# The first spreading of a graph kernel: five buffers of evicted rows, and slot numbers and rows of x asked for further ahead

## The chip, the cores and the metric

The kernel runs on one core of a Trainium2 chip. The metric is the device time of one execution in microseconds (us). The core has five engines that matter here: TensorE (PE, matrix multiplications; PEld are its weight loads), VectorE (DVE), ScalarE (ACT), GpSimd (POOL) and SyncE (SP, which here only issues transfers), and 16 DMA engines, which move data between the main memory (DRAM) and the on-chip memory (SBUF). TensorE writes its results into PSUM, from where VectorE or ScalarE copies ("evicts") them into SBUF.

## The reference

Two layers of a graph network over N = 32768 nodes with D = 128 features and E = 524288 edges, src to dst. Both need sums over edges:

```python
src, dst = edge_index
agg = jax.ops.segment_sum(x[src], dst, num_segments=N)      # layer 0
h = (1.0 + eps) * x + agg
h = relu(h @ W_loc1 + b_loc1) @ W_loc2 + b_loc2
h_local = _bn(x + h, g1, beta1)
... attention over 64 blocks of 512 nodes, feed-forward, norms
for _ in range(3):                                          # layer 1
    ... attention to 512 keys
    agg = zeros_like(x).at[row].add((dinv[:, None] * x)[col])
    x = 0.5 * x + 0.5 * (retrieved - 0.2 * (x - dinv[:, None] * agg))
```

The case concerns the first half of layer 0's `x[src]`: bringing every row of x to the places where the edges that start at it will be summed.

## The kernel before

**The exchange.** A sum over edges is done in two halves. The nodes are cut into NW = 256 windows of P = 128. In the first half, the *spreading*, each window of 128 source rows is multiplied with 0/1 matrices, so that rows come out in the order in which the receivers want them. Each window has 2 x KS = 12 groups of 128 slots (SL = 1536 slots). Edges that find no place in this grid are fetched one by one in the second half. In the second half, each receiving window loads its slots and sums them with other 0/1 matrices. The spread rows go through a DRAM array, `slots_d`, of 256 windows x 1.18 MB, in bf16; a float32 row is carried as three bf16 parts, hence ROW = 3 x 128 = 384 elements.

**The stages.** First comes half of layer 0's attention with the sorting of edges beside it, then the stage of this case, `spread_x` (L1812 to L1886), then a small verdict (`grid.verdict`, whether all edges fit) on which a branch depends, and then `layer0_grid` and `layer1_grid`. `layer0_grid` sums what spread_x wrote, and `layer1_grid` has its own spreadings, which use the same helper `Exchange.spread` from pools of two buffers.

**One window in spread_x.** The order of all instructions is written out by hand (`tc.manual_schedule`), and each engine works through its own in that order. For window w, of block b = w // 4, `ex.spread` runs for m = 0 to 5 (L1443 to L1456):

- two matmuls (L1448) of one group of 128 slots each, from the 0/1 matrix `picks[w]` and the three bf16 parts of the window's rows, into a PSUM tile `exp`, of which there are three;
- one eviction of both groups (L1453) into `y_o`, a tile of 2 x 6 x 384 bf16 elements in each of 128 partitions, that is 9216 bytes. Mostly ScalarE does it; VectorE does m = 2 of all windows and m = 5 of odd ones, that is 3 of 12 in a pair;
- after m = 2 and after m = 5, a store of half of `y_o` to `slots_d` (L1456), issued by SP. The pool `l0e` has two buffers of `y_o`, so the first eviction of window w cannot start before both stores of window w-2 have landed.

The 0/1 matrix of the *next* window is made by VectorE in between. A `row_of` transfer (L1833 to L1838) copies the 1536 slot numbers of one window from a row in DRAM to all 128 partitions, as a `band` (384 KB in SBUF). For odd windows VectorE compares the whole band at once with the partition number (`pick_b`, L1844), after m = 1. For even windows TensorE spreads 512 slot numbers at a time over the partitions (`row_p`, L1423) and VectorE compares them in PSUM (`pick`, L1848), after m = 1, 3 and 5. `row_of(w + 2)` is called at the start of odd w; its pool has two band buffers.

`load(b)` (L1823) asks for a block of four windows of x (256 KB, `xe`, three buffers), at the start of block b-2. ScalarE and VectorE split each block into its three bf16 parts during the block before (`split_steps`, L1386 to L1399), and SP stores these to a table. SP issues the loads of x, the bands, the stores of slots and the stores of the table, in program order, on one queue.

**Beside it** runs a sort of the edges that found no place (`sort_on`, `grid.build_more`), metered at 0.28 us of estimated VectorE time for each m. Its steps are VectorE's min and max over `more_a` and `more_b` (L96, L98), with some transposes.

Of the kernel before, what the change touches and what calls it, by code (L numbers as in the profile page):

```python
# [9 lines left out]
F32 = mybir.dt.float32  # L10
I32 = mybir.dt.int32
BF16 = mybir.dt.bfloat16
# [8 lines left out]
P = 128  # L21
D = 128
BLK = 512
NCH = BLK // P
# [7 lines left out]
KS = 6  # L32
# [10 lines left out]
ROW = 3 * D  # L43
# [866 lines left out]
def tile_gnn_resnorm(ctx: ExitStack, tc: tile.TileContext, a: dict, out: bass.AP):  # L910
# [68 lines left out]
    w = {}  # L979
# [342 lines left out]
    SL = 2 * KS * P  # L1322
# [5 lines left out]
    def grid_consts(pool):  # L1328
        gc["iota1"] = pool.tile([P, P], BF16, name="iota1")
        nc.vector.tensor_scalar(gc["iota1"], iota, 1.0, None, op0=OP.add)  # L1330
        gc["lane1"] = pool.tile([P, 1], F32, name="lane1")
        nc.vector.tensor_scalar(gc["lane1"], lane_f, 1.0, None, op0=OP.add)
        gc["down"] = pool.tile([P, P], BF16, name="down")
        nc.vector.tensor_copy(gc["down"], gc["lane1"].to_broadcast([P, P]))
        gc["ident"] = pool.tile([P, P], BF16, name="ident_b")
        nc.vector.tensor_copy(gc["ident"], ident)

    def rows_of(t, i):

        return t.rearrange("(b c p) d -> b p c d", c=NCH, p=P)[i]  # L1340
# [14 lines left out]
    class Exchange:  # L1355
# [8 lines left out]
        def __init__(self, key, slots, table):  # L1364
            self.grid, self.slots, self.table = grid.out[key], slots, table
            self.width = table.shape[1]
            self.bands = {}

        def load_rows(self, pool):
            self.row = pool.tile([P, 2, SL], BF16, name="row")  # L1370
            nc.sync.dma_start(self.row.rearrange("p h f -> p (h f)"), self.grid["row"])
# [71 lines left out]
        def spread(self, wp, pp, tag, w, pick, r, m, st, to_dve):  # L1443

            ps = pp.tile([P, 2, BLK], F32, name="exp", tag=tag)
            for j in range(2):
                o = (2 * m + j) * P
                nc.tensor.matmul(ps[:, j, :ROW], pick[:, o:o + P], r, start=True, stop=True)  # L1448
            if m == 0:
                st["y"] = wp.tile([P, 2, KS, ROW], BF16, name="y_o")  # L1450
            y = st["y"]
            dst = y.rearrange("p h r d -> p (h r) d")[:, 2 * m:2 * m + 2, :]
            (nc.vector.tensor_copy if to_dve else nc.scalar.copy)(dst, ps[:, :, :ROW])  # L1453
            if m % 3 == 2:
                h = m // 3
                nc.sync.dma_start(self.slots[h][:, w, :], y[:, h].rearrange("p r d -> p (r d)"))  # L1456
# [355 lines left out]
    def spread_x():  # L1812

        ex = Exchange("dst", slots_d[1], rows_d[T_STEPS])
        with tc.tile_pool(name="l0r", bufs=1) as gp, tc.tile_pool(name="l0e", bufs=2) as wp, \
                tc.tile_pool(name="l0e_p", bufs=2, space=PSUM) as p_k, \
                tc.tile_pool(name="l0e_e", bufs=3, space=PSUM) as p_e:
            grid_consts(gp)
            ex.load_rows(gp)
            xb, rows, ends, picks, bands, y = {}, {}, {}, {}, {}, {}  # L1820
            more = {"steps": grid.build_more(lane, Bank(p_k, "row_p")), "quota": 0.0}

            def load(b):  # L1823
                if b < NB:
                    xb[b] = wp.tile([P, NCH, D], F32, name="xe", bufs=3)
                    nc.sync.dma_start(xb[b], rows_of(a["x"], b))

            def split(b):
                if b < NB:
                    x = xb.pop(b)  # L1830
                    rows[b], ends[b] = ex.split_steps(wp, b, x, x)

            def row_of(w):  # L1833

                if w < NW:
                    bands[w] = wp.tile([P, SL], BF16, name="band")
                    src = ex.grid["row"][w % P:w % P + 1, w // P * SL:(w // P + 1) * SL]
                    nc.sync.dma_start(bands[w], src.to_broadcast([P, SL]))  # L1838

            def pick(w, j):  # L1840
                if w < NW and w % 2:
                    if j == 0:
                        picks[w] = wp.tile([P, SL], BF16, name="pick_b")
                        nc.vector.tensor_scalar(picks[w], bands.pop(w), gc["lane1"], None, op0=OP.is_equal)  # L1844
                elif w < NW:
                    if j == 0:
                        picks[w] = wp.tile([P, SL], FP8, name="pick")
                    nc.vector.tensor_scalar(picks[w][:, j * BLK:(j + 1) * BLK], ex.listed_row(p_k, "row_p", w, j),  # L1848
                                            gc["lane1"], None, op0=OP.is_equal, saturate=False)

            def sort_on():

                more["quota"] += MORE
                while more["steps"] is not None and more["quota"] > 0:
                    us = next(more["steps"], None)
                    if us is None:
                        more["steps"] = None
                    elif us < 0:
                        more["quota"] = 9 * us * MORE
                    else:  # L1860
                        more["quota"] -= us

            with tc.manual_schedule():
                load(0)
                load(1)
                split(0)
                for f in ends.pop(0):
                    f()
                row_of(1)
                for j in range(SL // BLK):  # L1870
                    pick(0, j)
                for w in range(NW):
                    b, c = divmod(w, NCH)
                    if w % 2:
                        row_of(w + 2)
                    if c == 0:
                        load(b + 2)
                        split(b + 1)
                    for m in range(KS):
                        ex.spread(wp, p_e, "exp", w, picks[w], rows[b][:, c, :], m, y, m == 2 or (m == 5 and w % 2))  # L1880
                        if m % 2:
                            pick(w + 1, m // 2)
                        if m == 3 and b + 1 in ends:
                            ends[b + 1][c]()
                        sort_on()
                for _ in more["steps"] or ():  # L1886
                    pass
# [125 lines left out]
    def layer1_grid(v_d, s3, c3):  # L2013

        exs = [Exchange("src", slots_d[t % 2], rows_d[t]) for t in range(T_STEPS)]
        with tc.tile_pool(name="l1g", bufs=1) as gp:
# [79 lines left out]
            def emit(t, b, st, wp, p_e, p_s, p_tr, share):  # L2096
# [39 lines left out]
                def spread(n):  # L2136
# [5 lines left out]
                    if m == KS - 1:  # L2142
                        del picked[i]

                places = [(n, lambda n=n: spread(n)) for n in range(NCH * KS)]
                return places + [(0, lambda: scores(0)), (3, lambda: scores(1)), (5, lambda: turn(0)),
                                 (6, lambda: scores(2)), (8, lambda: turn(1)), (9, lambda: scores(3)),
# [145 lines left out]
    with tc.tile_pool(name="atg", bufs=1) as gp, tc.tile_pool(name="ata", bufs=2) as ap, \  # L2293
# [4 lines left out]
        with tc.manual_schedule():  # L2298
# [13 lines left out]
            for us in edges or ():  # L2312
                pass
    spread_x()
    grid.verdict(flag)

# [47 lines left out]
```

## Time and profile before

| | |
|---|---|
| median of three runs | 13041.76 us (13023.18 to 13044.78) |
| the profiled execution | 13037.29 us |
| its span in the profile | 13035.5 us |
| mean granted TensorE clock, whole span | 0.947 |
| first L1448 matmul of spread_x | starts at 2344.3 us |
| last L1453 eviction of spread_x | ends at 3577.1 us |
| spread_x between these | 1233 us, VectorE busy 1081.7, ScalarE 928.2, TensorE 823.4 us, DMA share 0.89, 323 GB/s |
| first slots asked for by layer0_grid (L1461) | 3601.6 us |

The profile is of one execution. A line of a wait list names the engine and line that waited, then what it waited for; then follow the total of these waits in us, their number, and the longest. A line of the timeline has the start and the duration in us, the engine, the line, the operation, what it writes and reads, the number of merged instructions and, in brackets, how long the engine stood idle before it and what ended that. A line of stretches has the stretch, its length, the busy time and number of instructions of each engine, the granted TensorE clock (1.00 is full speed), the mean busy share of the 16 DMA engines (it passes 1 a little in places) and the GB/s that they moved.

The durations of one instruction in the stage, as the profile has them:

| line | engine | what | count | mean |
|---|---|---|---|---|
| L1453 | ACT | eviction into y_o, 128x768 | 1152 | 811 ns, less where they follow each other closely |
| L1453 | DVE | the same | 384 | 950 ns |
| L1848 | DVE | pick from row_p, 128x512 | 383 | 745 ns |
| L1844 | DVE | pick_b from a band, 128x1536 | 128 | 614 ns |
| L1448 | PE | exp, 128x384 | 3072 | 344 ns |
| L1423 | PE | row_p, 128x512 | 382 | 409 ns |

### The profile page before, as it was taken

What the parts mean: (1) busy time and instruction counts of PE and PEld (TensorE: products, weight loads), DVE (VectorE), ACT (ScalarE), POOL (GpSimd) and SP (SyncE); (2) the same over time, 40 slices, a digit from 0 to 9 for tenths busy, and PEclk for the clock granted to TensorE, in tenths of its full rate; (3) what the DMA queues carried; (4) which work ended last, traced back from release to release, by engine and by line L of the source; (5) the groups of instructions that cost most, each with busy time, mean ns of one, the idle gap of its engine ahead of it and who ended that gap; (6) DMA issues with size and microseconds to landing.
All of it is one profiled execution on the core that took longest, in us unless ns stands there. A gap on an engine that the chain in (4) does not pass through costs nothing. (4 is left out here: it accounts for less than half of the span.)

```text
span 13035.5 us, 164718 instructions
## 1 busy us (share of the span) xinstructions
PE 11183.2 (86%) x57832; PEld 5535.3 (42%) x57832; DVE 9515.6 (73%) x15195; ACT 6579.4 (50%) x10238; POOL 6154.3 (47%) x5525
## 2 busy tenths in 40 slices
PE   7798798666689999989997999999899999866666
PEld 2233233232244444444443555555455555433333
DVE  7978977798778888688886666666566666566666
ACT  4455355677723333478885666666566666500000
POOL 0083085000077777100003666666566666577777
PEclk9899899899999999999999999999999999987787
DMA  1000000788899999678888999999999999988887
GB/s 43 11 14 20 10 15 19 257 325 324 328 323 341 335 343 343 234 283 309 310 307 312 403 399 400 399 395 400 350 401 398 397 398 400 362 291 290 291 289 253
DMA packets 1410556, 3689.71 MB, mean 283 GB/s; under 512 B 219826, under 2 KB 634706, under 8 KB 1408562
## 3 DMA queue, kind: packets, MB, share of 16 engines
q1 hardware_dynamic: 969712, 2969.23, 60.2%
q0 software_dynamic: 252608, 520.41, 12.4%
q10 hardware_dynamic: 187394, 189.42, 4.4%
q8 instruction: 458, 7.50, 0.2%
q14 instruction: 384, 3.15, 0.1%
HBM read 2175.76 MB, written 1502.58 MB: 282 GB/s over the span
## 5 line engine op out<-in xcount | busy, mean ns | idle before, releaser
L1470 POOL DMA_INDIRECT listed<-rows,other x5120 | 5146.5, 1005 | 4164.4 <-issue 3156.1
L1453 ACT CAST y_o<-exp 128x768 bf16<-128x768 f32 x4224 | 3233.0, 806 | 1148.2 <-PE exp L1448 790.5
L1495 PEld LDWEIGHTS <-oh 128*128 128x128 bf16 x19456 | 1973.3, 102 | 2489.3 <-issue 1421.8
L1448 PE MATMUL exp<-rows,pick 128*128 128x384 bf16 x10752 | 2420.8, 327 | 385.2 <-ACT y_o L1453 223.0
L1495 PE MATMUL seg<-y_i,oh 128*128 128x384 bf16 x12288 | 2565.5, 345 | 21.0 <-DMA y_i<-slots 19.8
L1453 DVE CAST y_o<-exp 128x768 bf16<-128x768 f32 x1920 | 1830.3, 953 | 678.4 <-PE exp L1448 558.1
L1495 PE MATMUL seg<-listed,oh 128*128 128x384 bf16 (+1 forms) x5120 | 1242.6, 335 | 676.4 <-DMA listed<-rows,other 616.1
L1448 PEld LDWEIGHTS <-pick 128*128 128x128 fp8e4 x10752 | 1044.8, 98 | 1728.2 <-issue 1160.3
L1661 ACT ACTIVATE pT<-s 128x1024 f32<-128x1024 f32 x1024 | 1048.6, 1025 | 1174.2 <-PE s L1636 824.8
L2181 DVE SCALAR_TENSOR_TENSOR part_i<-seg,dinv,part_i 128x128 f32<-128x128 f32 x1536 | 531.5, 346 | 1337.5 <-PE seg L1495 1320.6
L1641 DVE TENSOR_REDUCE mx<-s 128x2 f32<-128x1024 f32 x1024 | 1245.4, 1220 | 278.6 <-PE s L1636 266.1
L1657 PE MATMUL s<-ql,k 32*128 32x512 f32 x4096 | 1220.8, 674 | 165.8 <-DVE mx L1641 153.5
L1636 PE MATMUL s<-k,q 32*128 32x512 f32 x4096 | 1220.0, 675 | 16.9 <-ACT pT L1661 10.9
L1084 ACT ACTIVATE ln_rs<-ln_mv,eps_c 128x4 f32<-128x4 f32 x128 | 38.0, 297 | 1638.9 <-DVE ln_mv L1082 1638.9
L2106 PE MATMUL s<-keysT,qT 128*128 128x512 f32 x1536 | 793.7, 598 | 2.1 <-ACT pr L1063 1.4
L1481 DVE TENSOR_TENSOR oh<-iota,slot 128x2432 bf16<-128x2432 bf16 x512 | 724.6, 1415 | 3.0 <-DMA slots<-y_o 3.0
L1481 DVE TENSOR_TENSOR oh<-ramp_p,slot 128x2432 bf16<-128x2432 bf16 x512 | 722.1, 1411 | 3.5 <-DMA slots<-y_o 3.4
L2118 PE MATMUL s<-pt,values 128*128 128x512 f32 x1536 | 720.4, 594 | 2.1 <-ACT pt L2113 2.0
L1495 PE MATMUL seg<-common,oh 128*128 128x384 bf16 (+1 forms) x2048 | 612.3, 347 | 49.4 <-DMA common<-rows,shared 49.2
L1657 PEld LDWEIGHTS s<-ql,k 32*128 32x128 f32 x4096 | 322.3, 192 | 701.5 <-DVE mx L1641 311.9
L1392 POOL MEMSET rows<- 128x8 bf16 x64 | 6.8, 107 | 1263.4 <-PE exp L1448 664.1
L1061 DVE TENSOR_REDUCE nm<-s 128x1 f32<-128x512 f32 x768 | 522.8, 683 | 107.9 <-PE s L2106 105.5
(410 smaller groups left out, 14333.8 us busy)
## 6 DMA issues: line engine op xcount, KB each, us to landing
slots<-y_o SPq DMA_DIRECT2D x2048, 576.0 KB
y_i<-slots SPq DMA_DIRECT2D x1024, 1152.0 KB
pick<-pick SPq DMA_DIRECT2D x1024, 192.0 KB
listed<-rows,other POOLq DMA_INDIRECT x5120
rows<-rows SPq DMA_DIRECT2D x192, 384.0 KB
band<-row_dst SPq DMA_DIRECT2D x128, 384.0 KB
band<-row_src ACTq DMA_DIRECT2D x256, 192.0 KB
part_d<-part_o SPq DMA_DIRECT2D x192, 256.0 KB
```

What stands on the lines that cost most here:

```text
L1448: nc.tensor.matmul(ps[:, j, :ROW], pick[:, o:o + P], r, start=True, stop=True)
L1453: (nc.vector.tensor_copy if to_dve else nc.scalar.copy)(dst, ps[:, :, :ROW])
L1470: nc.gpsimd.indirect_dma_start(out=g[:, k, :], out_offset=None, in_=self.table, in_offset=bass.IndirectOffsetOnAxis(ap=index[:, k:k + 1], ...
L1481: nc.vector.tensor_tensor(oh.rearrange("p c (w z) -> p c w z", z=2), ramp.rearrange("p (w z) -> p w z", z=2)[:, None].to_broadcast([P, NC2 ...
L1495: nc.tensor.matmul(ps[:, :n], oh[:, j, :], src, start=(k == 0), stop=(k == NC2 - 1))
L1636: nc.tensor.matmul(ps[:, s % 2, :], t["q", o][32 * s:32 * s + 32, c * P:(c + 1) * P], t["k", o][32 * s:32 * s + 32, :], start=True, stop=True)
L1641: nc.vector.tensor_reduce(m[:, c, 2 * i:2 * i + 2, xr[o]], st[b].pop(("two", i)), AX.X, OP.max, negate=True)
L1657: nc.tensor.matmul(ps[:, s % 2, :], t["k", o][32 * s:32 * s + 32, c * P:(c + 1) * P], t["ql", o][32 * s:32 * s + 32, :], start=True, stop= ...
L1661: nc.scalar.activation(t["p", c][:, 2 * i:2 * i + 2, :], ps, AF.Exp)
L2106: nc.tensor.matmul(s, st["q"][:, c * P:(c + 1) * P], keysT, start=True, stop=True)
L2118: nc.tensor.matmul(ps, values[:, k, :], st["pt"][:, k, :], start=(k == 0), stop=(k == NCH - 1))
L2181: nc.vector.scalar_tensor_tensor(dst, ps[:, o * D:(o + 1) * D], dinv01[:, i:i + 1], acc, op0=OP.mult, op1=OP.add)
```

## The change

The Exchange gets a field `kept`, the number of `y_o` buffers, 2 for all but spread_x, where it is 5. In spread_x, the blocks of x have four buffers in place of three and are asked for at the start of block b-3 in place of b-2. The bands have three buffers in place of two and are asked for four windows ahead in place of two. At the start, three blocks and two bands are asked for in place of two and one. No computation changes.

```diff
@@ class Exchange @@
             self.bands = {}
+            self.kept = 2
...
             if m == 0:
-                st["y"] = wp.tile([P, 2, KS, ROW], BF16, name="y_o")
+                st["y"] = wp.tile([P, 2, KS, ROW], BF16, name="y_o", bufs=self.kept)
@@ def spread_x @@
         ex = Exchange("dst", slots_d[1], rows_d[T_STEPS])
+        ex.kept = 5
...
-                    xb[b] = wp.tile([P, NCH, D], F32, name="xe", bufs=3)
+                    xb[b] = wp.tile([P, NCH, D], F32, name="xe", bufs=4)
...
-                    bands[w] = wp.tile([P, SL], BF16, name="band")
+                    bands[w] = wp.tile([P, SL], BF16, name="band", bufs=3)
...
-                load(0)
-                load(1)
+                for b in range(3):
+                    load(b)
                 split(0)
                 for f in ends.pop(0):
                     f()
                 row_of(1)
+                row_of(3)
...
                 for w in range(NW):
                     b, c = divmod(w, NCH)
                     if w % 2:
-                        row_of(w + 2)
+                        row_of(w + 4)
                     if c == 0:
-                        load(b + 2)
+                        load(b + 3)
                         split(b + 1)
```

## The prediction

> **What bounds the kernel now.** I read first the page's 40 slices, to find the stretch that the change touches. All of its lines lie in spread_x, whose first L1448 matmul starts at 2344.3 us and whose last eviction (L1453, the copy of `exp` into `y_o`) ends at 3577.1 us: 1233 us of the 13035.5 us span, 256 windows, so 4.82 us for a window and 9.63 us for a pair. No other stage asks for the changed buffers, so only this one can move, and what follows it starts when it ends.
>
> Then I asked for the busy time of each engine in two stretches of this stage: the one in which a sort (`more_a`, `more_b`) runs on VectorE beside the spreading, up to 3200 us, and the rest.
>
> ```profile
> core 0: us, PE busy (x) PEld busy (x) DVE busy (x) ACT busy (x) POOL busy (x), PEclk, DMA share, GB/s
> 2350.00:3200.00 850.00, 563.53 (x2600) 256.95 (x2600) 799.02 (x999) 639.03 (x906) 4.69 (x44) 0.95 0.88 320
> 3200.00:3577.00 377.00, 255.81 (x1111) 114.12 (x1108) 280.49 (x477) 284.99 (x407) 7.64 (x24) 0.91 0.89 331
> ```
>
> In the first stretch VectorE is busy 799 of 850 us (94%): it is the bound there, with 51 us of idle time left to take. In the second no engine is above 76%, and the largest figure is the DMA share, 0.89. Third, the waits of VectorE in the first stretch, and those of ScalarE in the whole stage (2344 to 3577 us):
>
> ```profile
> DVE pick L1848 <- PE row_p L1423: 28.8, 38, 2.9
> DVE pick_b L1844 <- DMA band<-row_dst: 14.2, 23, 1.7
> DVE y_o L1453 <- DMA slots<-y_o: 2.7, 4, 1.0
> ```
> ```profile
> ACT y_o L1453 <- PE exp L1448: 165.6, 211, 8.6
> ACT y_o L1453 <- DMA slots<-y_o: 118.2, 106, 4.0
> ```
>
> ScalarE stands 118 us waiting until a store of `y_o` has landed, so that the buffer may be written again. Fourth, the timeline shows how that reaches VectorE:
>
> ```profile
> 3565.86 2.91 ACT L1453 CAST y_o<-exp 128x768 bf16<-128x768 f32 x4 [2.01 <-DMA slots<-y_o]
> 3565.89 0.96 DVE L1453 CAST y_o<-exp 128x768 bf16<-128x768 f32 x1 [0.48 <-DMA slots<-y_o]
> 3566.72 0.48 PE L1448 MATMUL exp<-rows,pick_b 128*128 128x384 bf16 x2 [1.77 <-ACT y_o L1453]
> ...
> 3567.04 0.38 PE L1423 MATMUL row_p<-row,ident_b 128*128 128x512 bf16 x1
> ...
> 3567.45 0.75 DVE L1848 TENSOR_SCALAR pick<-row_p,lane 128x512 fp8e4<-128x512 f32 x1 [0.61 <-PE row_p L1423]
> ```
>
> The first ScalarE eviction waits 2.01 us for a store; the three `exp` banks stay full, so TensorE waits 1.77 us; the `row_p` matmul stands behind it in TensorE's order, so VectorE's next `pick` waits 0.61 us. Last, whether the DMA engines could do more:
>
> ```profile
> 3750.00:5250.00 1500.00, 1441.45 (x8460) 704.41 (x8460) 1294.39 (x1820) 462.92 (x788) 1115.80 (x1179) 1.00 0.99 341
> 7250.00:9000.00 1750.00, 1705.22 (x8803) 956.09 (x8802) 1080.65 (x1750) 1118.72 (x1853) 1148.24 (x1090) 1.00 1.03 399
> ```
>
> Later stages hold shares of 0.99 and 1.03 for 1500 us and more, so 0.88 is not full.
>
> **The change part by part.** It adds and removes no instruction: the same 512 stores, 128 bands and 64 blocks of x, some asked for earlier. What can change is who waits.
>
> (1) Five `y_o` buffers. The eviction of window w now waits for the stores of window w-5, not of w-2. At 4.82 us a window that is 19 us after the last store of that window was issued, against 4.82 us. The longest such wait is 4.0 us, so as long as the DMA engines keep up on average, all of it goes. In the sort's stretch this is worth VectorE's idle time only: its own 2.7 us, and that part of the 28.8 us behind `row_p` that comes from stores. I followed each of these 38 waits back in the timeline: 19 of them, 12.7 us, come within 3 us of a ScalarE wait for a store; the others may descend from an older one or from VectorE's own late evictions (67.5 us of TensorE waits there are put to those). Bounds 12.7 and 28.8 us; I take 16, near the lower end, because only that is seen. Sum of this part in this stretch: 2.7 + 16 = 18.7 us.
>
> (2) Bands asked two pairs ahead. Asked at 2800.18 us, a band is used at 2806.22 us in this trace: some 6 us. The new place, two windows earlier, makes it 6 + 9.6 = 15.7 us. The 14.2 us of waits in the sort's stretch have a longest of 1.7 us, so all go: 14.2 us. The bounds are 14.2 and 0, the latter if the queue ahead of the band grows as much as its lead.
>
> Both together in the sort's stretch: 18.7 + 14.2 = 32.9 us; the ceiling is the idle 51 us.
>
> (3) The second stretch. Direct stalls of VectorE are more there (bands 18.1 us, slots 8.7 us, `row_p` 59.4 us), but the engine work is no bound; the transfers are. 377 us at 0.89 is 335.5 us of full transfer time, so the ceiling is 41.5 us. The engines that feed the stores will still leave gaps, so I do not take 1.0; with 0.96, between the present 0.89 and the later 0.99 to 1.03 and nearer to these, it takes 335.5 / 0.96 = 349.5 us: 27.5 us won. Bounds 0 and 41.5.
>
> (4) Blocks of x one further ahead. In the whole stage only one wait for x is recorded, the first load (10.7 us, before the stage has started), so I put this at nothing. What hides it now is a lead of a full block, four windows or 19 us. It costs something at the start: a third x load (256 KB) and a second band (384 KB) are issued before the first windows. At the stage's 323 GB/s they are 640 KB, 2.0 us, of which the first load of x needs only part. I take 1 us, bounds 0 and 2.
>
> On SP's queue nothing waits because of the new places: the buffer that a band takes (three of them, asked at window w for w+4) held band w-2, read in window w-3; that of an x block held b-1, split in block b-2. In both cases, as before, the reader is long done. The waiting instruction on SP stays L1456 (802 us behind evictions), which costs nothing as it waits for work.
>
> (5) The end. The verdict, the branch and the next stage's table loads follow. Before, the last eviction ends at 3577.1 us and the slot table has landed at 3590.5 us. If the backlog of stores is two windows deeper when evictions end, 2 x 1.18 MB at 323 GB/s is 7.3 us later by that clock. I take 4 us of it, bounds 0 and 7.3 (up to 11 if three deeper).
>
> Sum: 32.9 + 27.5 - 1 - 4 = 55.4 us. The profiled execution took 13037.29 us (span 13035.5), so 12981.9; the median of the runs is 13041.76, 4.5 us above it, which gives **12,986 us**. Lower limit by the ceilings: 51 + 41.5 = 92.5 us, 12,949.
>
> **The rivals.** *A, more than that.* VectorE fills nearly all its idle time and the transfers run at 1.0. For it: TensorE's granted clock falls to 0.50 in single 2 us samples after such stalls, which would go too. Against it: VectorE's late evictions remain. Between 75 and 92 us, about 12,958.
>
> *B, the stalls move rather than go.* ScalarE's 118 us of waits lie on an engine that is 75% busy; VectorE may still wait for `row_p` because only three `exp` banks couple the engines. Then I keep 14.2 us of bands and 2.7 us of slots in the first stretch, and some 10 us in the second, less 5 us: 22 us, 13,020, within what can be told from no change. For it: the larger ScalarE wait, 165.6 us, is for TensorE and not for stores. Against it: 19 of 38 waits follow a store.
>
> *C, the queue in front of the bands, slower.* Stores, bands, blocks, split rows and the sort's own tables all go out on SP's one queue (88.0 of the 89% share). With five buffers up to four finished windows of stores can stand ahead of a band: 4 x 4.82 = 19.3 us at the present pace, against a lead of 15.7 us, so a band would come 3.6 us late when the backlog is full. It decides from a mean wait of `pick_b`: what the other parts win, 18.7 + 27.5 - 5 = 41 us, plus the present 36.1 us of band waits, over 128 bands, is 0.60 us each. At 1.0 us each: 128 - 36.1 - 41 = 51 us slower, 13,093. For it: bands make VectorE wait 47 times already, with a lead of 6 us. Against it: at a share of 0.88 to 0.96 the backlog is not full for long, and VectorE's waiting lets it drain.
>
> The Trainium skill, "DMA: Bandwidth & Descriptors", section "Queues, rings and completion order", says that each DMA engine takes the descriptors of a ring in the ring's order; that is rival C's premise and speaks against deeper stores on the queue of the bands. By that rule alone, with the backlog always full, an estimate is 128 bands each 3.6 us late, 461 us of waits, and 13,426 us. The present waits, 0.28 us on average over 128 bands with a longest of 3.8 us, agree with a band that stands behind one or two stores; no run here shows a deeper queue yet.
>
> *D, the change does nothing.* Were the engines' transfers full at 0.89 for this mixture, the time would stay at 13,042. The later stages speak against it, and 2 us samples between 2600 and 2700 us go from 0.33 to 1.06, so gaps are there.
>
> **How the numbers follow.** Something like 0.2% (26 us) is about what a measurement of this kernel can tell from no change: faster is below 13,016, slower above 13,068. Chances: the forecast 0.58 (its own range 12,960 to 13,012), A 0.12, B 0.18, C 0.08, D 0.04. Faster: 0.58 + 0.12 + 0.07 of B = 0.77; same: 0.11 of B and 0.04 = 0.15; slower 0.08. The range reaches from the lower limit, less some 4 us for the spread of the runs (13023 to 13045), to where B ends: 12,945 to 13,035. It leaves out C, D and little more.
>
> **What would show it.** The stage, from first matmul to last eviction, should take some 1172 us, 4.6 us a window: about 817 us where the first stretch took 850, with VectorE at 97 to 98% busy, and about 350 us where the second took 377, with the DMA share at 0.95 or above. ScalarE's waits for stores should fall from 118 us to below 20, `pick_b` waits from 36 to below 10. Busy times in later stages should stay. If stores no longer stop ScalarE but the VectorE's idle time in the stage stays near its 151 us (1233 less 1081.7 busy), B holds; if `pick_b` waits pass 77 us in all, C; if ScalarE's store waits stay, D. The prediction is wrong if the stage's time falls by less than 30 us or more than 85.

## The result, and the profile after

The changed kernel takes 12975.53 us (median of 6 runs, 12969.33 to 13000.94), the kernel before in 6 runs 13043.81 us: a ratio of 0.9952, 95% interval 0.9941 to 0.9963, that is 48 to 77 us less. The forecast was 12,986 us.

The profiled execution has a span of 12972.1 us. In it the stage runs from 2335.5 us (first exp matmul) to 3509.5 us (last eviction); from the first to the last exp matmul it takes 1172.7 us, against 1231.4 before. All stage times below are of this second kind. The sort's end (the store of the sorted table, at 3204.4 us before and 3166.7 us after) cuts it into 860.1 and 371.3 us before, 831.2 and 341.5 us after. (The changed kernel's lines lie one to three higher: L1449 exp, L1454 eviction, L1846 pick_b, L1850 pick.)

The busy times in the two stretches, after:

```profile
core 0: us, PE busy (x) PEld busy (x) DVE busy (x) ACT busy (x) POOL busy (x), PEclk, DMA share, GB/s
2341.00:3162.00 821.00, 572.07 (x2556) 256.67 (x2598) 793.57 (x999) 638.45 (x906) 4.67 (x44) 0.93 0.91 331
3162.00:3509.50 347.50, 242.42 (x1092) 109.45 (x1110) 275.29 (x477) 284.81 (x408) 7.63 (x24) 0.95 0.94 357
```

VectorE went from 94% to 96.7% busy in the first stretch, the DMA share from 0.89 to 0.94 in the second. What VectorE and TensorE waited for in the whole stage, before:

```profile
DVE pick L1848 <- PE row_p L1423: 88.2, 91, 3.4
DVE pick_b L1844 <- DMA band<-row_dst: 36.1, 47, 3.8
```
```profile
PE exp L1448 <- DVE rows L1395: 41.3, 47, 2.1
```

What VectorE, ScalarE and TensorE waited for there, after:

```profile
DVE pick L1850 <- PE exp L1449: 42.8, 26, 3.8
DVE pick L1850 <- PE row_p L1424: 37.9, 31, 2.4
DVE pick_b L1846 <- DMA band<-row_dst: 3.6, 1, 3.6
```
```profile
ACT y_o L1454 <- PE exp L1449: 166.4, 203, 8.1
ACT y_o L1454 <- issue: 48.6, 25, 3.2
...
ACT y_o L1454 <- DMA slots<-y_o: 5.1, 7, 1.1
```
```profile
PE exp L1449 <- ACT y_o L1454: 193.8, 524, 1.0
PE exp L1449 <- DVE rows L1396: 68.0, 53, 2.4
```

The waits for stores are gone from ScalarE (118.2 to 5.1 us), those for bands from VectorE (36.1 to 3.6 us; the one left is the first band of all). What VectorE still waits for comes from TensorE: 80.7 us in two lines, against 88.2 before. TensorE waits 68 us for the split rows of the next block (the three bf16 parts that `split_steps` makes; 41.3 us before): remember that line. ScalarE's 48.6 us under "issue", idle time for which the profile names no cause, were not there before. They go with the late split and not with stores: whole_split, below, has the same buffers with an earlier split, and 6.6 us of them.

Of the profiles' difference of 63.4 us, 58.7 us lie in the stage. Another 8.8 us lie ahead of it and are not the change's: the attention ahead of the stage ran faster near its end. The same four score matmuls took half the time there, and the granted clock from 2300 to 2330 us was 0.55 before and 0.90 after. The kernel before, and the changed one:

```profile
2310.61 2.08 PE L1657 MATMUL s<-ql,k 32*128 32x512 f32 x4
```
```profile
2311.48 1.13 PE L1658 MATMUL s<-ql,k 32*128 32x512 f32 x4
```

These two make 67.5 us, so 4.1 us are given back behind the stage. From the first slots asked for to the end the changed kernel took 5.0 us longer than the kernel before, with the same code; the eight other kernels that were profiled on chips of this speed took 2.5 to 24.8 us longer there. So this is not put down to the change.

In the other kernels below, which are the same up to there, the first exp matmul starts anywhere between 2330.8 and 2350.2 us. Single spans are therefore compared by their stage, and times by ratios of many runs.

### The profile page after: what moved, and what is told of

Same layout as the page of the kernel before. It is cut to its first block, busy times and chain, and to the rows that moved or that the text cites. A ratio compares the mean times of both kernels' runs of the same rounds, so it can differ in the third digit from the quotient of the medians.

```text
span 12972.1 us, 164426 instructions
## 1 busy us (share of the span) xinstructions
PE 11179.1 (86%) x57769; PEld 5526.2 (43%) x57832; DVE 9506.6 (73%) x15195; ACT 6578.9 (51%) x10238; POOL 6158.7 (47%) x5525
## 3 DMA queue, kind: packets, MB, share of 16 engines
q0 software_dynamic: 252608, 520.41, 12.5%
## 5 line engine op out<-in xcount | busy, mean ns | idle before, releaser
L1454 ACT CAST y_o<-exp 128x768 bf16<-128x768 f32 x4224 | 3228.1, 805 | 1092.3 <-PE exp L1449 778.5
L1449 PE MATMUL exp<-rows,pick 128*128 128x384 bf16 x10752 | 2425.8, 328 | 404.7 <-ACT y_o L1454 241.0
L1454 DVE CAST y_o<-exp 128x768 bf16<-128x768 f32 x1920 | 1830.5, 953 | 674.9 <-PE exp L1449 548.7
L1449 PEld LDWEIGHTS <-pick 128*128 128x128 fp8e4 x10752 | 1041.6, 98 | 1757.4 <-issue 1111.3
L1063 ACT ACTIVATE pr<-s,nm 128x512 f32<-128x512 f32 x768 | 536.4, 698 | 114.3 <-DVE nm L1061 111.1
```

What stands on the lines that cost most here:

```text
L1063: nc.scalar.activation(pr, s, AF.Exp, bias=nm, accum_out=sums)
```

## The experiments

**Each part alone.** Five buffers of `y_o`, and nothing else:

```diff
+        ex.kept = 5          # bands: bufs=2, row_of(w + 2); x: bufs=3, load(b + 2)
```

> Five buffers of y_o alone; bands and blocks of x asked for as before. Theory (stores stop ScalarE, bands stop VectorE, each for itself): ScalarE's waits for stores fall from 118 us to under 10, the bands' waits of 36 us stay or grow a little, the stage spread_x (first L1448 matmul to last eviction, 1233 us before, 1174 with the whole change) takes 1190 to 1205 us, and the time is 30 to 45 us below that of before. Rival C (the queue): with more stores ahead of each band the waits of pick_b pass 80 us and the time is within 10 us of before, or above it; then the bands' lead would be what makes the buffers pay.

Measured: ratio 0.9988 (0.9979 to 0.9997), some 16 us less; the stage 1214.8 us, 16.6 us less, half of what was expected. ScalarE's waits for stores fell to 9.7 us, as expected, but VectorE waited for bands twice as long as before:

```profile
DVE pick_b L1846 <- DMA band<-row_dst: 71.2, 62, 3.7
DVE pick L1850 <- PE row_p L1424: 28.5, 30, 2.4
DVE pick L1850 <- PE exp L1449: 24.5, 24, 3.0
```

The waits behind TensorE fell from 88.2 to 53.0 us; 35.1 us of bands came in their place, 49.7 of the 71.2 us in the 366 us after the sort. It looks like rival C, short of the 80 us set for it. But the traces show hardly a deeper queue. A band is 128 packets of 3072 bytes, a size that no other transfer of the stage has, so the packet records of a trace tell when each band began and when it landed. Medians over the bands, with stores counted by their packets that were issued and had not begun:

| | stores ahead of a band at its issue | issue to last packet, us | issue until VectorE is ready for it, us |
|---|---|---|---|
| kernel before, whole stage | 1.95 | 5.64 | 6.18 |
| five buffers, whole stage | 1.95 | 5.73 | 5.97 |
| kernel before, after the sort | 1.75 | 5.39 | 5.70 |
| five buffers, after the sort | 1.96 | 5.87 | 4.90 |

Rival C counts on up to four windows, eight stores, ahead of a band; some two stood there, as before. A band took a little longer to land, and VectorE, no longer held up by stores, came for it sooner. In sum the last packets come 17.8 us too late before and 47.9 us with five buffers. An estimate from these records, band by band: the shorter time until VectorE is ready would by itself have made it 40.4 us, the slower landing by itself 30.2.

The bands two windows earlier, and nothing else:

```diff
-                        row_of(w + 2)
+                        row_of(w + 4)          # and bufs=3, row_of(3) at the start
```

> Bands asked for two windows earlier, with three buffers; two buffers of y_o and three of x as before. Theory: pick_b's waits go from 36 us to under 5, ScalarE's waits for stores stay at some 118 us; in the stretch with the sort VectorE wins up to 14 us, in the stretch after it little, because stores still stop the evictions. The stage takes 1212 to 1225 us, the time is 8 to 20 us below before. Rival (the bands' waits only cover waits for stores): ScalarE's waits for stores grow by as much, and the time is within 5 us of before.

Measured: ratio 0.9990 (0.9981 to 1.0000), some 13 us; the stage 1222.7 us, 8.7 us less. The waits of VectorE, and of ScalarE for stores:

```profile
DVE pick L1848 <- PE row_p L1423: 74.9, 76, 3.7
DVE pick L1848 <- PE exp L1448: 31.9, 19, 3.6
DVE y_o L1453 <- DMA slots<-y_o: 16.3, 19, 2.1
DVE pick_b L1844 <- DMA band<-row_dst: 3.8, 1, 3.8
```
```profile
ACT y_o L1453 <- DMA slots<-y_o: 128.1, 113, 3.0
```

Of the 32.3 us of band waits taken away, 18.6 us are back behind TensorE (88.2 to 106.8 us), 4.9 us at VectorE's own evictions (11.4 to 16.3), and ScalarE's waits for stores grew by 9.9 us. The stage and the time came out as the theory had it, and the rival is half right: a band's wait and a store's wait often cover the same time.

The blocks of x one block earlier, alone (`bufs=4`, `load(b + 3)`, three loads at the start):

> Blocks of x asked for one block earlier, with four buffers, and three at the start; the rest as before. Theory: no wait for x is recorded before, so nothing: the stage stays within 4 us of 1233 us and the time within 10 us of before. Rival (the load of x, four windows before its use, stands behind stores and delays the split rows): TensorE's waits for the split rows (L1395, 41 us before) fall by half and the stage by 10 us or more.

Measured: ratio 0.9997 (0.9988 to 1.0006), the stage 1229.9 us, TensorE's waits for the split rows 39.5 against 41.3 us. Nothing, as the theory has it.

So the singles bring 16.6, 8.7 and 1.5 us of the stage, 26.8 in all, and the whole 58.7. Is the surplus due to buffers and bands together, or to x?

```diff
+        ex.kept = 5
+                    bands[w] = wp.tile([P, SL], BF16, name="band", bufs=3)
+                        row_of(w + 4)          # x as before
```

> Five buffers of y_o and the bands two windows earlier, the blocks of x as before. Alone the two gave 17 and 9 us of the stage, together with x 59. Theory (each alone leaves the other's wait in its place, so they pay together): the stage is within 6 us of the whole change's 1173 us (first matmul to last matmul), and the time 50 to 68 us below before; the blocks of x add nothing. Rival (the blocks of x, too, come late behind deeper stores, and the surplus over the single gains is theirs): the stage takes 1190 us or more and waits for x or for the split rows appear.

Measured: ratio 0.9948 (0.9935 to 0.9962), the stage 1173.6 us (831.8 and 341.8). That is the whole change; x adds nothing to it either. Buffers and bands, 16.6 and 8.7 us alone, bring 57.8 us together.

**Why the bands come late: SP's queue or full DMA engines?** The buffers alone again, with the bands at their old place in the program, but issued by ScalarE:

```diff
-                    nc.sync.dma_start(bands[w], src.to_broadcast([P, SL]))
+                    nc.scalar.dma_start(bands[w], src.to_broadcast([P, SL]))
```

> Five buffers of y_o, bands asked for at the old place with the old two buffers, but on ScalarE's queue in place of SP's; x as before. With the bands on SP's queue they made VectorE wait 71 us in the stage. Queue theory (a band waits behind the stores that were issued before it on the same queue): the waits fall below 25 us and the stage, 1215 us with the bands on SP's queue, takes 1180 to 1200 us; the issues take some 0.5 us of ScalarE each, 64 us in all, which it has. Rival (the DMA engines are full, and a band is slow on any queue): the waits stay at 50 us or more and the stage above 1205 us.

Measured: ratio 0.9962 (0.9948 to 0.9976), the stage 1185.1 us, 29.7 us less than with the bands on SP's queue. VectorE, whole stage:

```profile
DVE pick L1850 <- PE row_p L1424: 57.0, 61, 2.9
DVE pick L1850 <- PE exp L1449: 32.6, 22, 3.5
...
DVE pick_b L1846 <- DMA band<-row_dst: 2.8, 5, 1.0
```

The same transfers on the same 16 engines no longer come late, 2.8 us in place of 71.2, at a DMA share that is no lower (0.90 and 0.93, against 0.89 and 0.90). So it was not that the DMA engines were full. But two things changed at once, as one band of only_y and one of this kernel show, each from its issue to its use:

```profile
2549.68 0.89 SPq L1840 DMA_DIRECT2D band<-row_dst  x1
...
2555.88 0.62 DVE L1846 TENSOR_SCALAR pick_b<-band,lane 128x1536 bf16<-128x1536 bf16 x1
```
```profile
2542.18 0.33 ACTq L1840 DMA_DIRECT2D band<-row_dst  x1
...
2549.72 0.61 DVE L1846 TENSOR_SCALAR pick_b<-band,lane 128x1536 bf16<-128x1536 bf16 x1
```

First, the band is issued earlier. SP comes to it after the last store of the window before, for which it waits until the eviction has ended: it issued the band 1.42 us after that window's last ScalarE eviction had begun (median). ScalarE's queue issued it 0.43 us before that eviction began, although the eviction stands ahead of it in the program. So the time from issue until VectorE is ready went from 5.97 to 7.90 us. Second, the band lands sooner: 4.44 us after its issue in place of 5.73, with its first packet after 1.22 us in place of 3.04, and with 0.57 stores ahead of it in place of 1.95. An estimate as above: with the earlier issue alone 3.3 of the 47.9 us would be left, with the sooner landing alone 25.6. So what delayed the bands lay in the order on SP, and by this estimate more in SP's late issue than in the transfers in front; no run here separates the two. (ScalarE's issues took 0.33 us each, 42 us in all, not the 64 us expected.)

The Trainium skill, "DMA: Bandwidth & Descriptors", section "Queues, rings and completion order", says that a ring's descriptors are taken in order and that an engine goes round the rings that have work. The sooner first packet agrees with it. The Trainium skill says on the same page, "Issuing engines are not separate DMA queues", that a second issuing engine only saves sequencer time. The earlier issue can be counted as that; the landing that came 1.3 us sooner cannot, and there the measurement decides.

**How many buffers.** The whole change with `ex.kept = 3`:

> The whole change, but three buffers of y_o in place of five. Theory: the eviction then waits for stores issued two windows (9.6 us) earlier, against a longest wait of 4.0 us with one window, so ScalarE's waits for stores are under 15 us, and the stage takes 1174 to 1184 us; the time within 10 us of that of the whole change, some 55 to 68 us below before. Rival (the depth is used up in the stretch after the sort, where transfers are the bound): the stretch after the sort, 342 us with five, takes 352 us or more and ScalarE waits over 30 us for stores.

Measured: ratio 0.9959 (0.9945 to 0.9972); the stage 1179.0 us (833.3 and 345.7), ScalarE's waits for stores 5.5 us. The intervals of three and five overlap: one buffer more does nearly all of it, and what the last two add, 6.3 us in single profiles, is not settled. (The time, some 53 us below before, is just short of the 55 to 68 expected.)

**What bounds the stage now.** First, relieve VectorE while the sort runs:

```diff
-  ..., m, y, m == 2 or (m == 5 and w % 2))
+  ..., m, y, m == 2 or (m == 5 and w % 2 and more["steps"] is None))
```

> The whole change, and as long as the sort runs, ScalarE does the evictions of m = 5 that VectorE did in odd windows: VectorE keeps one eviction of six. Theory (VectorE, 97% busy, is the bound while the sort runs; the transfers at a share of 0.91 have room): per pair 0.95 us of VectorE go, ScalarE gets 0.75 to 0.81 us more (from 78% to some 90%); the stretch with the sort, 831 us, takes 775 to 800 us, with the DMA share at 0.94 or above, the stretch after it stays at 342 us; the time is 25 to 50 us below that of the whole change, 12925 to 12950 us. Rival (the stretch is bound by the chain of eviction and matmul, or by transfers, not by VectorE): the stretch stays above 820 us, with VectorE at 87%.

Measured beside y_and_bands on the same chip: ratio 0.9918 (0.9904 to 0.9932), a median of 12950.80 us against 12991.08, 40 us less; the stage 1118.2 us. VectorE was the bound with the sort; the transfers had room and took it (831 to 784.5 us there). The stretch after the sort, which the edit leaves alone, was expected to stay at 342 us and took 333.7; why is open.

```profile
2347.20:3131.70 784.50, 553.89 (x2585) 255.80 (x2628) 726.39 (x919) 698.45 (x1007) 4.68 (x44) 0.96 0.95 350
3131.70:3467.00 335.30, 238.11 (x1076) 108.96 (x1093) 247.26 (x444) 296.73 (x429) 7.74 (x24) 0.95 0.97 366
```

Then the line of TensorE's waits for split rows, which stands in this kernel too:

```profile
PE exp L1449 <- DVE rows L1396: 68.2, 53, 2.6
```

The last of the four split steps is VectorE's, at m = 3 of a block's last window, two steps before the block ends; whenever VectorE is late there, TensorE waits:

```diff
-                        if m == 3 and b + 1 in ends:
-                            ends[b + 1][c]()
+                        if b + 1 in ends and (c, m) in ((0, 3), (1, 0), (1, 3), (2, 3)):
+                            ends[b + 1].pop(0)()
```

> As act_in_sort, and the four steps that split the next block are done earlier: at m = 3 of its first window, m = 0 and 3 of the second and m = 3 of the third, in place of m = 3 of each of the four. In the whole change TensorE waited 68 us for the last of them. Theory (bound by VectorE or transfers, so TensorE's waits cost nothing): those waits fall below 15 us, and the time is within 6 us of act_in_sort's. Rival (with VectorE relieved these waits are on the path): 10 us or more below act_in_sort.

The theory is refuted: 12890.69 us, ratio 0.9878 (0.9862 to 0.9893), 60 us below act_in_sort; the stage 1067.9 us, 50.3 us less.

```profile
2345.70:3093.70 748.00, 541.98 (x2587) 251.82 (x2630) 722.27 (x920) 700.56 (x1009) 4.69 (x44) 0.99 0.99 368
3093.70:3415.00 321.30, 235.75 (x1073) 109.71 (x1091) 248.85 (x443) 294.72 (x427) 7.75 (x24) 0.95 1.00 379
```

The DMA share is 0.99 and 1.00: only now the transfers are full from end to end, and with the sort VectorE is 97% busy beside them. TensorE's wait for the split rows, 1.3 us on average and at most once in a block, had left gaps behind it: VectorE's waits behind TensorE fell from 119.5 to 56.8 us. Is such a wait free while VectorE is the bound, as was thought? The split alone, on the whole change:

> The whole change with the earlier split of the next block, VectorE's evictions as they were. In act_in_sort the earlier split took 36 us from the stretch with the sort (784 to 748 us) and 14 us from the rest (334 to 320 us). Theory (while VectorE, 97% busy, is the bound, TensorE's waits for the split rows cost little): the stretch with the sort, 831 us, stays at 815 us or more, VectorE at 98 to 99%, and the rest falls from 342 to some 325 us; the time is 20 to 35 us below the whole change. Rival (the late split is a stall of its own, whatever the bound): 780 us or less in the stretch with the sort, 50 us or more in all.

Measured on a chip on which the kernel before takes 14331.40 us (below): ratio 0.9938 (0.9917 to 0.9958), the stage 1143.3 us (819.5 and 323.8), 29.4 us less than the whole change on its chip. The ratios of the two overlap, so this rests on the profiles of the stage.

```profile
2350.20:3169.70 819.50, 577.52 (x2586) 261.93 (x2629) 797.50 (x1008) 654.72 (x919) 4.68 (x44) 0.93 0.92 336
3169.70:3495.00 325.30, 233.12 (x1075) 108.59 (x1093) 270.53 (x471) 278.52 (x399) 7.64 (x24) 0.96 0.98 373
```

With the sort it gives 11.7 us, with VectorE still at 97%; with VectorE relieved, the same edit gave 36.5 us. After the sort it gives 17.7 us, as the transfers fill up (0.94 to 0.98). So the theory holds for this kernel, though such a wait is cheap there and not free; it failed where VectorE had been relieved.

Last, both later edits on the kernel before, without anything of this change:

> The kernel before (two buffers of y_o, bands and blocks of x at their old places) with the shifted evictions and the earlier split, so without anything of this change. With this change they brought the stage to 1068 us. Theory (waits for stores and bands stay, some 118 and 36 us or more, and are now on the path of ScalarE, which does five evictions of six): the stage takes 1150 us or more, the DMA share stays below 0.95, the time is 12960 us or above. Rival (the two edits alone fill the transfers, and the deeper buffers are not needed for it): the stage takes 1100 us or less.

Measured on the same chip as whole_split: ratio 0.9996 (0.9981 to 1.0010), nothing; the stage 1219.8 us. VectorE's and ScalarE's waits:

```profile
DVE pick_b L1844 <- DMA band<-row_dst: 151.5, 100, 4.0
```
```profile
ACT y_o L1453 <- DMA slots<-y_o: 116.0, 97, 3.6
```

Without the buffers and the earlier bands, what the two edits free goes into waits for bands, four times as long as before. The bands land as before (a median of 5.63 us after their issue, against 5.64), but VectorE is ready for them after 4.80 us in place of 6.18. The change of this case pays 59 us of the stage by itself, and the two edits, which bring another 105 us behind it, bring next to nothing without it.

## Why the prediction was right, and where its steps were not

*What bounds the kernel.* VectorE with the sort, transfers without: both held in the main. act_in_sort shows the first (831 to 784.5 us when VectorE is relieved); for the second, the share rose to 0.94 in this change and on to 1.00. VectorE came to 96.7% and the share to 0.94, both just below what was set as a sign (97 to 98%, and 0.95).

*(1) and (2), buffers and bands, 18.7 + 14.2 = 32.9 us with the sort.* The sum was near (28.9 measured, start included), two of its steps were not. The first is the 16 us taken for waits behind `row_p`. VectorE's waits behind TensorE in this stretch, 28.8 us before, are after the change:

```profile
DVE pick L1850 <- PE row_p L1424: 14.8, 17, 2.0
DVE pick L1850 <- PE exp L1449: 7.5, 8, 3.2
```

That is 6.5 us less, and not 16. The 2.7 and 14.2 us went as said. Another 5.1 us came from where the prediction had no term: VectorE's own busy time with the sort fell from 805.3 to 800.2 us (the last paragraph below has more). The second is that each part was priced as if it could be had alone. Alone the buffers brought 11.3 us (860.1 to 848.8) and the bands 3.6 us (to 856.5) there; y_and_bands, with both, 28.3. The prediction summed the direct waits of one engine by what ended them, but one wait stands in front of another: without the store's wait the band's comes into view, and the other way round. That holds more strongly after the sort.

*(3), the second stretch, 27.5 us at a share of 0.96.* Measured 29.8 us at 0.94, and the match is in part luck. By the prediction's own sum, with the transfer time at a full share fixed, 0.94 would have given 371.3 x 0.89 / 0.94 = 351.5 us, 19.8 us won. But 331 GB/s at 0.89 became 357 at 0.94, so the same share moved some 2% more, and about 1% fewer bytes fell into this stretch; why is not shown. Here the buffers alone give 5.3 us, the bands 5.1 us, and both 29.5 us. The step from 0.94 to 0.98 came with the earlier split, which the prediction did not have: the line of waits for the split rows (41.3 us) was in the profile before, and the prediction does not name it.

*(4), x.* Nothing, as said, in only_x and in y_and_bands. The start cost nothing that can be seen either: the first load of x ends ScalarE's wait 3.2 us after its issue, against 3.0 before.

*(5), the end, 4 us lost.* Wrong: nothing is lost. The slot table's copy begins 12.5 us after the last eviction (13.4 before), and the first slots are asked for 23.6 us after it (24.5). So no deeper backlog of stores shows at the end. After the change:

```profile
3508.56 0.96 DVE L1454 CAST y_o<-exp 128x768 bf16<-128x768 f32 x1 [0.34 <-PE exp L1449]
...
3522.03 11.09 DVE L1381 COPY slot<-slot 128x4864 bf16<-128x4864 bf16 x2 [4.94 <-DMA slot<-slot_dst]
...
3533.15 1.39 SPq L1462 DMA_DIRECT2D y_i<-slots  x3
```

*The rivals.* A did not come: VectorE still idles 27 us with the sort. B, that the stalls move, is what the buffers alone or the bands alone show. C, that deeper stores delay the bands, came in small part only: with five buffers some two stores stood ahead of a band as before, and it landed 5.73 us after its issue against 5.64. The bands' waits in only_y, 71.2 us and near the 77 us from which C would hold, come more from the shorter time until VectorE is ready; C's sign could not tell the two apart.

That the full change lies near the forecast owes something to chance: a loss at the end that did not come, a smaller gain behind TensorE, and a joint effect that a sum of separate parts happened to match. The bands' longer lead, which the prediction credited with 14.2 us in the stretch with the sort, is worth 17.0 us there beside five buffers (848.8 to 831.8), but only 3.6 without them (860.1 to 856.5).

## What to carry to other kernels

Waits of two kinds that alternate must be taken away together; test each alone and you may drop both. An engine that no longer waits for stores comes sooner for its next load: ask for the loads earlier, or let another engine issue them, in the same edit. And a short wait that comes once a block is cheap only as long as some engine is nearly full; look at it again after each change of the bound.

## What the runs showed of the hardware

One chip of those used ran its three kernels some 10% slower (the kernel before at a median of 14331.40 us), although the two kernels profiled on it took 1143.3 and 1219.8 us for the stage, less than the kernel before on the first chip. A loss is seen in the later stages: between 4000 and 5000 us its 16 DMA engines moved 270 GB/s at a share of 0.83 in whole_split, against 340 GB/s at 0.99 in the kernel before on the first chip. Why is open; of the times, only ratios are compared across chips here.

VectorE's busy time in the stage fell from 1081.7 to 1070.7 us with the same instructions. In the changed kernel a pick of 0.74 us at 3495.60 us is followed by pick_b at 3496.26, 0.66 us later: when instructions stand ready, the next starts before the last has ended, by this trace, so a full VectorE does a little more than the durations of single instructions say.
